# Softmax attention in slots of four heads and 64 queries, with the probabilities turned by VectorE in 32x32 squares

## The chip, the core and the metric

The program runs on one core of a Trainium2 chip. A core has five engines that work beside each other, each through its own instructions in their order: TensorE (PE in the profile, its weight loads PEld), VectorE (DVE), ScalarE (ACT), GpSimd (POOL) and SyncE (SP, which here only issues DMAs). TensorE reads SBUF and writes PSUM, which has eight banks of 512 fp32 values a partition; GpSimd works on SBUF alone here. The metric is the device time of one execution in microseconds (us). All data are fp32 but for one small bf16 product of the scan.

## The reference

Two residual blocks on x of shape (8, 1024, 512), eight sequences of 1024 tokens. The second block (a gated state-space scan) isn't touched by the change. The first one is modulated attention with 16 heads of 32 channels:

```python
x = x * s1[:, None, :]                                  # styles, then a norm over the channels
x = (x - mu) * rsqrt(var + EPS_IN)
q = heads((x @ q_weight.T) * q_dc);  k = heads((x @ k_weight.T) * k_dc)
v_flat = (x @ v_weight.T) * v_dc * s2;  v = heads(v_flat)
attn = softmax(einsum('bhqd,bhkd->bhqk', q, k) * d ** -0.5, axis=-1)
out = einsum('bhqk,bhkd->bhqd', attn, v)                # back to (B, S, H)
return (out @ w_weight.T) * w_dc + (v_flat @ u_weight.T) * u_dc      # x = x + this
```

## The kernel before

**Blocks and slots.** `modulated_attention` runs over 32 blocks (b, o): a sequence b and a group o of four heads, whose 4 x 32 channels fill the 128 partitions. `project` makes q, k and v of a block in a layout with channels on partitions and the 1024 tokens along the free axis. A block has 16 slots (`SB = 2 * NQ`), so there are 512. A slot is 128 queries (`q`, one of eight) of two of the four heads (`pair`).

**One slot.** `scores` (L292, L295) makes for each of the two heads a tile of 128 queries (on partitions) by 1024 keys, in two matmuls of 512 keys; a head has 32 channels, so a matmul uses 32 of TensorE's 128 rows. So that four matmuls use four different row groups, copies of q and k shifted by 64 partitions (`q2`, `k2`, made in `project` by DMAs on SP) serve the second 512 keys. The two tiles take four PSUM banks (`ps_s`), and the next slot takes the same ones. VectorE finds the negative maximum of each row (L465, one instruction for each head), ScalarE exponentiates with it as bias and adds up the rows (L475, one for each head), VectorE inverts the sums (`rinv`) and GpSimd multiplies the probabilities by them (L480, L489, L494).

**Turning.** The product with the values needs keys on partitions. One slot later `flip` turns each head's 128x1024 probabilities by eight TensorE transposes of 128x128 into PSUM (L302); ScalarE copies the first head's to SBUF (L472), VectorE the second's (L486, L491).

**Weighing.** Every second slot `weigh` (L309) takes the four heads of one q: for each of eight groups of 128 keys and each head one matmul with the head's 32 value channels as weights and the 128 turned probabilities moving, four column groups of TensorE beside each other. VectorE copies the result out (L454).

**Background work.** Between these, slots run pieces of generators: `project` for the next block, the output products `out_u` and `out_w` (all through `chain`, L136: four matmuls of 128x128x512 in a row, then an evacuation, by ScalarE for q, k and v, by VectorE for the outputs), the turning of the next x (`turn`) and its norm (`aside`). A piece is one matmul of a chain. `due` says how many pieces a slot owes (40 or 44 a block), and `late` how many of them come after the slot's own work. `turn_values` turns v by TensorE, and ScalarE copies it to `vt` (L237).

The order is written by hand (`tc.manual_schedule()`): every engine gets its instructions in the order of the code, and waits where a tile isn't ready. In fp32 a matmul of the code appears as two MATMUL and two LDWEIGHTS instructions in the profile (transposes as one of each).

After the attention, `gated_scan` runs the second block, with VectorE's custom step (L951), ScalarE's weighing (L929) and the DMAs that fan rows out (L919) as its largest parts.

Of the kernel before, what the change touches and what calls it, by code (L numbers as in the profile page):

```python
# [8 lines left out]
F32 = mybir.dt.float32  # L9
BF16 = mybir.dt.bfloat16  # L10
AF = mybir.ActivationFunctionType
ALU = mybir.AluOpType
AX = mybir.AxisListType
# [3 lines left out]
P = 128  # L17
# [4 lines left out]
HD = H // NH  # L22
# [7 lines left out]


@with_exitstack
def modulated_attention(ctx, tc, const, xp, tok, x1_d, xu_d, S, x, xT, cond, wT, ident, condT, early, handover):

# [6 lines left out]
    nc = tc.nc  # L43
    HW = S // 2
    KT = S // P
# [13 lines left out]
    eps = own.tile([P, 1], F32, name="eps_h")  # L59
    nc.vector.memset(eps, EPS)  # L60
    dc = own.tile([P, 5, KH, B], F32, name="dc")
    small = ctx.enter_context(tc.tile_pool(name="small", bufs=6))
    ps_m = ctx.enter_context(tc.tile_pool(name="ps_m", bufs=2, space=PSUM))

# [131 lines left out]
    def project(ws, xh, b, o, st, steps=STEPS):  # L196

        if not st:
            st["q"] = ring.tile([P, S], F32, tag="qT", name="qT")
            st["k"] = ring.tile([P, S], F32, tag="kT", name="kT")  # L200
            st["q2"] = ring.tile([P, S], F32, tag="q2", name="q2")
            st["k2"] = ring.tile([P, HW], F32, tag="k2", name="k2")
            st["v"] = ring.tile([P, S], F32, tag="vT", bufs=5, name="vT")
        qT, kT, q2, k2, vT = (st[n] for n in ("q", "k", "q2", "k2", "v"))

        def moved(dst, src):
            nc.sync.dma_start(out=dst[64:128], in_=src[0:64])
            nc.sync.dma_start(out=dst[0:64], in_=src[64:128])

        for name, hf in steps:  # L210
            c = half(hf)

            def q_out(ps):
                nc.scalar.mul(qT[:, c], ps, qdc[:, o, b : b + 1])
                moved(q2[:, c], qT[:, c])

            def k_out(ps):
                nc.scalar.mul(kT[:, c], ps, kdc[:, o, b : b + 1])
                if hf == 1:
                    moved(k2, kT[:, c])  # L220

            def v_out(ps):
                nc.scalar.mul(vT[:, c], ps, vdc[:, o, b : b + 1])
                ready.append((st, hf))

            out = {"q": q_out, "k": k_out, "v": v_out}[name]
            yield from chain([(ws[name][:, k], xh[hf][:, k]) for k in range(KH)], out)

    def turn_values():

        st, hf = ready.pop(0)
        if hf == 0:
            st["vt"] = ring.tile([P, KT, P], F32, tag="vt", name="vt")
        ps = ps_t.tile([P, 4, P], F32, tag="t", name="t_ps")
        for j in range(4):
            nc.tensor.transpose(ps[:, j], st["v"][:, (4 * hf + j) * P : (4 * hf + j + 1) * P], ident)
        nc.scalar.copy(st["vt"][:, 4 * hf : 4 * hf + 4], ps)  # L237

    def load_xr(src, o, hf):
        xr = ring.tile([P, HW], F32, tag="xr", bufs=3, name="xr")  # L240
# [39 lines left out]

    def scores(st, q, pair):


        s_ps = [ps_s.tile([P, S], F32, tag="s", name="s_ps") for _ in range(2)]
        qc = slice(q * P, (q + 1) * P)
        for hf in range(2):
            for i in range(2):
                if hf == 0:  # L290
                    r = slice(64 * pair + i * HD, 64 * pair + (i + 1) * HD)
                    nc.tensor.matmul(s_ps[i][:, 0:HW], st["q"][r, qc], st["k"][r, 0:HW], start=True, stop=True)  # L292
                else:
                    r = slice(64 * (1 - pair) + i * HD, 64 * (1 - pair) + (i + 1) * HD)
                    nc.tensor.matmul(s_ps[i][:, HW:S], st["q2"][r, qc], st["k2"][r], start=True, stop=True)  # L295
        return s_ps

    def flip(pr, g):
        ps = ps_t.tile([P, 4, P], F32, tag="t", name="t_ps")
        for j in range(4):  # L300
            c0 = (4 * g + j) * P
            nc.tensor.transpose(ps[:, j], pr[:, c0 : c0 + P], ident)  # L302
        return ps

    def weigh(av, pT, vt):
        for kt in range(KT):
            for i in range(4):
                r = slice(i * HD, (i + 1) * HD)
                nc.tensor.matmul(  # L309
                    av[r], vt[:, kt, r], pT[:, i, kt], start=(kt == 0), stop=(kt == KT - 1),  # L310
                    skip_group_check=True,
                )

    blocks = [(b, o) for b in range(B) for o in range(KH)]
    sts = {bo: {} for bo in blocks}
    slots = [(bo, q, pair) for bo in blocks for q in range(NQ) for pair in range(2)]
    wts = {}

    def fetch_w(n):
# [84 lines left out]
    def aside(n):  # L404

        b, o = blocks[n]
        if b + 1 < B and o in (1, 2):
# [2 lines left out]
            yield  # L410
            yield from normalise(xs_next[o - 1])

    xs_next, xh_next, last_w = [], [], []
    PIECES = {0: 40, 1: 40, 2: 44, 3: 44}
    probs = None
    flipped = {}
    bg, side, ran, ripe = iter(()), iter(()), 0, 0
    for n in range(len(slots) + 2):
        bo, q, pair = slots[n] if n < len(slots) else (None, None, None)
        if n % SB == 0:  # L420
            for _ in bg:
                pass
# [8 lines left out]
        if bo is not None:  # L431

            done, pieces = n % SB + 1, (54, 29)[n // SB] if n < 2 * SB else PIECES[bo[1]]
            few = max(1, (pieces - 2 * NQ + NQ) // SB)
            due = few * (done - done // 2) + -(-(pieces - NQ * few) * (done // 2) // NQ) - ran
            if n < 3:
                due = 6
            if n // SB == len(blocks) - 1:
# [3 lines left out]
            ran += due  # L442


        m = (n - 3) // 2
        if n % 2 == 1 and m >= 0:
            mbo, mq, _ = slots[2 * m]
            while "vt" not in sts[mbo] or (sts[mbo], 1) in ready:
                turn_values()
            av = ps_t.tile([P, 4, P], F32, tag="t", name="t_ps")[:, 0]  # L450
            weigh(av, flipped.pop(m), sts[mbo]["vt"])
            if mq == 0:
                sts[mbo]["a"] = ring.tile([P, S], F32, tag="aT", bufs=6, name="aT")
            nc.vector.tensor_copy(sts[mbo]["a"][:, mq * P : (mq + 1) * P], av)  # L454
        elif ripe and ready:
            turn_values()
        ripe = len(ready) if n % 2 == 1 else 0
        fresh = None
        if bo is not None:
            s_ps = scores(sts[bo], q, pair)  # L460
            nmax = [small.tile([P, 1], F32, name="nmax") for _ in range(2)]
            rsum = [small.tile([P, 1], F32, name="rsum") for _ in range(2)]
            fresh = [pp.tile([P, S], F32, name="pr") for _ in range(2)]
            for i in range(2):
                nc.vector.tensor_reduce(nmax[i], s_ps[i], AX.X, ALU.max, negate=True)  # L465
        if probs is not None:
            if (n - 1) % 2 == 0:
                flipped[(n - 1) // 2] = two.tile([P, 4, KT, P], F32, name="pT")
            pT = flipped[(n - 1) // 2][:, 2 * ((n - 1) % 2) : 2 * ((n - 1) % 2) + 2]
            t_ps = [flip(probs[0], g) for g in range(2)]  # L470
            for g in range(2):
                nc.scalar.copy(pT[:, 0, 4 * g : 4 * g + 4], t_ps[g])  # L472
        if bo is not None:
            for i in range(2):
                nc.scalar.activation(fresh[i], s_ps[i], AF.Exp, bias=nmax[i], accum_out=rsum[i])  # L475
        if bo is not None:
            rinv = [small.tile([P, 1], F32, name="rinv") for _ in range(2)]
            if n % 2 == 1:
                nc.vector.reciprocal(rinv[0], rsum[0])
                nc.gpsimd.tensor_scalar(fresh[0], fresh[0], rinv[0], 1.0, ALU.mult, ALU.mult)  # L480
        late = (due + 1 - n % 2) // 2
        for _ in range(due - late):
            next(bg, None)
        if probs is not None:
            t_ps = [flip(probs[1], g) for g in range(2)]
            nc.vector.tensor_copy(pT[:, 1, 0:4], t_ps[0])  # L486
        if bo is not None and n % 2 == 0:
            nc.vector.reciprocal(rinv[0], rsum[0])  # L488
            nc.gpsimd.tensor_scalar(fresh[0], fresh[0], rinv[0], 1.0, ALU.mult, ALU.mult)  # L489
        if probs is not None:  # L490
            nc.vector.tensor_copy(pT[:, 1, 4:8], t_ps[1])  # L491
        if bo is not None:
            nc.vector.reciprocal(rinv[1], rsum[1])  # L493
            nc.gpsimd.tensor_scalar(fresh[1], fresh[1], rinv[1], 1.0, ALU.mult, ALU.mult)  # L494
        for _ in range(late):
            next(bg, None)
        next(side, None)
        probs = fresh
    for _ in last_w[0]:
        pass  # L500

# [553 lines left out]
def network(ctx: ExitStack, tc: tile.TileContext, S, ins, out):  # L1055
# [22 lines left out]
    with tc.manual_schedule():  # L1078
        modulated_attention(
            tc, const, xp, tok, x1_d, xu_d, S, ins["x"], ins["xT"], ins["cond"],  # L1080
            {n: ins[f"w{n}T"] for n in "qkvwu"}, ident, ins["condT"], early, handover,
        )
        gated_scan(
            tc, const, tok, x1_d, S, win, tables, ins["w_conv"], ins["b_conv_c"], ins["ln_g"], ins["ln_b"],
# [78 lines left out]
```

## Time and profile before

| what | value |
|---|---|
| device time, median of 3 runs | 5662.0 us (5652.78 to 5665.36) |
| the profiled execution's own time | 5657.36 us |
| its span, first to last instruction | 5655.6 us |
| TensorE busy | 5502.6 us (97%), 43312 matmuls |
| VectorE busy | 4375.3 us (77%) |
| ScalarE busy | 3920.6 us (69%) |
| GpSimd busy | 1567.2 us (28%) |
| granted TensorE clock, mean | 0.99 |

The profile is one execution, taken by the hardware profiler. A line of a group says: source line, engine, operation, what it writes and reads, shapes, how often (xN), then the busy time in us and the mean ns of one, then the engine's idle time just ahead of such instructions and what ended most of it. A matmul's end is modelled and matmuls overlap, so their busy time is a union and their mean is longer than the distance from one to the next. In the timeline, a line is a run of instructions of one form: start, length of the run, and xN how many. The attention takes about the first 3270 us of the span, and the scan the rest.

### The profile page before, as it was taken

To read this page: it belongs to the slowest core of one execution; us is meant where nothing else is said; L and a number is where in the kernel's file an instruction comes from. 1 tells how busy PE (TensorE), PEld (TensorE's weight loads), DVE (VectorE), ACT (ScalarE), POOL (GpSimd) and SP (SyncE) were. 2 spreads that over 40 slices of the span, in tenths; PEclk is the share of its full clock that TensorE was granted. 3 is DMA by queue.
4 is the path that set the end of the run, shared out by engine and by line. 5 is a ranking of instruction groups with operands and counts; after the bars stand their busy time and mean duration, and the time that the engine had idled before them with its cause. 6 is when DMAs were issued, how large, how long until landed. Compare 5 with 4: busy or idle time off the path is not lost.

```text
span 5655.6 us, 113681 instructions
## 1 busy us (share of the span) xinstructions
PE 5502.6 (97%) x43312; PEld 3172.9 (56%) x43312; DVE 4375.3 (77%) x6847; ACT 3920.6 (69%) x6953; POOL 1567.2 (28%) x1723
## 2 busy tenths in 40 slices
PE   7999999999999999999999989999999999999998
PEld 4566666666666666666666555555555555555553
DVE  4676666766766767766766669999999999999996
ACT  5555555555555555555555558988888888889886
POOL 2443433433434434434333311111111111111111
PEclk9999999999999999999999989999999999999999
DMA  2111212112212202112111258888888888888886
GB/s 82 38 53 35 55 53 56 43 45 55 53 37 66 56 22 74 53 32 60 53 36 35 88 149 230 238 236 238 236 237 239 238 235 235 236 233 238 235 235 186
DMA packets 377214, 714.83 MB, mean 126 GB/s; under 512 B 198320, under 2 KB 280512, under 8 KB 347488
## 3 DMA queue, kind: packets, MB, share of 16 engines
q1 hardware_dynamic: 346704, 684.81, 44.3%
q0 software_dynamic: 29968, 22.77, 1.5%
q8 instruction: 344, 5.64, 0.4%
q14 instruction: 198, 1.62, 0.1%
HBM read 596.66 MB, written 83.89 MB: 120 GB/s over the span
## 4 chain that ended last, share of the span: by engine, by line
PE 66%; DMA 15%; DVE 9%; ACT 5%; SPq 3%; issue 2%; POOL 0%; DVEq 0%; ACTq 0%; POOLq 0%
PE mm_ps L136 18%; PE t_ps L302 15%; DMA xb<-xd 11%; PE s_ps L292 9%; PE t_ps L309 9%; DVE h L951 4%; PE in_ps L686 4%; PE y_ps L938 3%; SPq L919 3%; PE g_ps L841 2%; DMA xd<-xt 2%; ACT xb L929 2%; PE o_ps L878 1%; DMA out<-o_sb 1%; PE fan_ps L899 1%
## 5 line engine op out<-in xcount | busy, mean ns | idle before, releaser
L465 DVE TENSOR_REDUCE nmax<-s_ps 128x1 f32<-128x1024 f32 x1024 | 1205.5, 1219 | 464.5 <-PE s_ps L295 464.3
L951 DVE CUSTOM_DVE_ANT_0 h<-h,xb,lim 128x1024 f32<-128x1024 f32 x1024 | 1372.1, 1340 | 98.2 <-ACT xb L929 40.5
L472 ACT COPY pT<-t_ps 128x512 f32<-128x512 f32 x1024 | 550.6, 589 | 1294.2 <-PE t_ps L302 1294.2
L302 PEld LDWEIGHTS t_ps<-ident,pr 128*128 128x128 f32 x8192 | 915.9, 141 | 649.5 <-issue 500.1
L929 ACT ACTIVATE xb<-xb,ws 128x1024 f32<-128x1024 f32 x1024 | 1178.1, 1164 | 54.4 <-DMA xb<-xd 34.8
L475 ACT ACTIVATE pr<-s_ps,nmax 128x1024 f32<-128x1024 f32 x1024 | 1140.8, 1128 | 6.0 <-DVE nmax L465 5.9
L302 PE MATMUL t_ps<-ident,pr 128*128 128x128 f32 x8192 | 1094.0, 277 | 8.0 <-ACT pT L472 4.6
L494 POOL TENSOR_SCALAR pr<-pr,rinv 128x1024 f32<-128x1024 f32 x512 | 574.3, 1122 | 131.4 <-DVE rinv L493 121.8
L292 PE MATMUL s_ps<-kT,qT 32*128 32x512 f32 x2048 | 586.6, 640 | 3.1 <-ACT pr L475 2.4
L295 PE MATMUL s_ps<-k,q 32*128 32x512 f32 x2048 | 577.1, 639 | 1.1 <-DMA q<-qT 1.1
L480 POOL TENSOR_SCALAR pr<-pr,rinv 128x1024 f32<-128x1024 f32 x256 | 287.4, 1123 | 1035.3 <-PE t_ps L302 956.7
L938 PE MATMUL y_ps<-h,yw 128*32 128x512 f32 x4096 | 529.8, 613 | 36.2 <-DVE y_ps L773 32.4
L309 PEld LDWEIGHTS t_ps<-pT,vt 128*32 128x32 f32 x16384 | 433.2, 110 | 204.2 <-DVE rinv L488 164.5
L309 PE MATMUL t_ps<-pT,vt 128*32 128x128 f32 x16384 | 502.6, 275 | 10.9 <-DVE pT L486 9.2
L489 POOL TENSOR_SCALAR pr<-pr,rinv 128x1024 f32<-128x1024 f32 x256 | 287.5, 1123 | 792.6 <-DVE rinv L488 744.9
L686 PE MATMUL in_ps<-x,win 128*128 128x256 f32 x2048 | 491.9, 386 | 4.1 <-ACT xb L910 4.1
L841 PE MATMUL g_ps<-win,x1t 128*128 128x512 f32 x1024 | 472.2, 604 | 3.6 <-ACT x1t L836 3.6
L878 PE MATMUL o_ps<-wout,xt 128*128 128x512 f32 x1024 | 458.5, 595 | 0.0
L890 POOL DMA_DIRECT2D out<-o_sb x256 | 150.9, 595 | 1054.4 <-ACT o_sb L884 954.3
L686 PEld LDWEIGHTS in_ps<-x,win 128*128 128x128 f32 x2048 | 376.8, 193 | 95.0 <-ACT xb L910 26.5
L804 POOL DMA_DIRECT2D bca<-few x256 | 129.0, 513 | 1021.8 <-ACT few L797 1016.2
L486 DVE COPY pT<-t_ps 128x512 f32<-128x512 f32 x512 | 352.3, 688 | 48.0 <-PE t_ps L302 48.0
(162 smaller groups left out, 6961.0 us busy)
## 6 DMA issues: line engine op xcount, KB each, us to landing
xb<-xd SPq DMA_DIRECT2D x1792, 256.0 KB
xd<-xt SPq DMA_DIRECT2D x64, 512.0 KB
q<-qT SPq DMA_DIRECT2D x128, 128.0 KB
xr<-in_xT SPq DMA_DIRECT2D x64, 256.0 KB
xu_d<-xr SPq DMA_DIRECT2D x64, 256.0 KB
xr<-xu_d SPq DMA_DIRECT2D x64, 256.0 KB
x_d<-xr SPq DMA_DIRECT2D x64, 256.0 KB
out<-o_sb POOLq DMA_DIRECT2D x256, 64.0 KB, 4.7
```

The costliest lines, as they stand in the source:

```text
L136: nc.tensor.matmul(ps, w, x, start=(k == 0), stop=(k == KH - 1))
L292: nc.tensor.matmul(s_ps[i][:, 0:HW], st["q"][r, qc], st["k"][r, 0:HW], start=True, stop=True)
L295: nc.tensor.matmul(s_ps[i][:, HW:S], st["q2"][r, qc], st["k2"][r], start=True, stop=True)
L302: nc.tensor.transpose(ps[:, j], pr[:, c0 : c0 + P], ident)
L309: nc.tensor.matmul(av[r], vt[:, kt, r], pT[:, i, kt], start=(kt == 0), stop=(kt == KT - 1), skip_group_check=True,)
L465: nc.vector.tensor_reduce(nmax[i], s_ps[i], AX.X, ALU.max, negate=True)
L475: nc.scalar.activation(fresh[i], s_ps[i], AF.Exp, bias=nmax[i], accum_out=rsum[i])
L686: nc.tensor.matmul(ps, win[kk][:, k * P : (k + 1) * P], st["x1"][:, kk].rearrange("p b t -> p (b t)"), start=(kk == 0), stop=False,)
L841: nc.tensor.matmul(ps, st["xo", i][:, k], win[k][:, DI + half * 512 : DI + (half + 1) * 512], start=(k == 0), stop=(k == KH - 1),)
L929: nc.scalar.mul(xbs[n], xbs[n], sts[c]["ws"][:, t : t + 1])
L938: nc.tensor.matmul(st["y", i][32 * r : 32 * r + 32, hf * 512 : (hf + 1) * 512], yws[i][:, 4 * q + r, :], hs[4 * g + r][:, hf * 512 : (hf + ...
L951: nc.vector._custom_dve(dve_ops.TENSOR_ADD_SAT, out=h, in0=last["h"], in1=xbs.pop(n), s0=lim[:, 0, t : t + 1], s1=lim[:, 1, t : t + 1],)
```

## The change

A slot becomes 64 queries (`s`, one of sixteen) of all four heads; there are still 512 slots, with as many scores in each.

- `scores`: the 1024 keys of a head are taken as 32 groups of 32; groups 0, 2, 4, ... are one half, groups 1, 3, 5, ... the other. Partition group g of the score tile holds 32 of the 64 queries (g // 2) and one half of the keys (g % 2). A matmul has 32 channels, 32 queries and 512 keys; 16 of them (four row groups by four column groups of TensorE) make a slot. `q2`, `k2` and their DMAs go.
- A row's keys now lie on two partitions, so each has a maximum and a sum of its own. `factors` takes the difference of the two maxima by a matmul with a constant (`pair[:, 0]`) into the PSUM of the first score tile, VectorE clips it at 0, ScalarE exponentiates it and GpSimd multiplies the sums; `total` adds the two sums by a second matmul (`pair[:, 1]`) in the next slot; `shares` inverts there, and GpSimd scales the probabilities, one instruction for each head.
- `turn_probs`: VectorE turns the probabilities from SBUF to SBUF in squares of 32x32, two instructions of 128x1024 a slot. TensorE's transposes and the copies out of PSUM go.
- `weigh`: after turning, each query half has 64 partitions, with 32 keys of each key half. For each of 16 pairs of key groups, two query halves and four heads there is one matmul with 64 rows, 32 columns and 64 moving columns (32 queries of two slots); eight such matmuls lie on eight tiles of TensorE, two row groups by four column groups. Values shifted by 64 partitions (`vm`) come by two DMAs on SP for each `turn_values`.
- `due` and `late`, and the order of a slot's steps, change with it.

```diff
-    def scores(st, q, pair):
...
+    def scores(st, s):
+        s_ps = [ps_s.tile([P, 2, HW], F32, tag="s", name="s_ps") for _ in range(2)]
+        for g in range(4):
+            half_q, half_k = divmod(g, 2)
+            q0 = 64 * s + HD * half_q
+            for h in range(4):
+                r = slice(h * HD, (h + 1) * HD)
+                keys = st["k"][r].rearrange("p (j a k) -> p a j k", a=2, k=HD)[:, half_k]
+                nc.tensor.matmul(
+                    s_ps[h // 2][g * HD : (g + 1) * HD, h % 2], st["q"][r, q0 : q0 + HD], keys, start=True, stop=True
+                )
         return s_ps
-    def flip(pr, g):
...
+    def weigh(av, pT, st):
+        for j in range(2 * KT):
+            for r in range(2):
+                rows = slice(64 * r, 64 * r + 64)
+                v = st["vt" if j % 2 == r else "vm"]
+                for h in range(4):
+                    c = slice(h * HD, (h + 1) * HD)
+                    nc.tensor.matmul(
+                        av[r][c, 0:64], v[rows, j // 2, c], pT[rows, h, :, j * HD : (j + 1) * HD],
+                        start=(j == 0), stop=(j == 2 * KT - 1), skip_group_check=True,
+                    )
...
+    def limits(ch, i):
+        if i == 0:
+            ch["nmax"] = small.tile([P, 4], F32, name="nmax")
+            ch["sum"] = small.tile([P, 4], F32, name="rsum")
+        for h in ((0, 1), (1, 2)) if i == 0 else ((0, 2),):
+            nc.vector.tensor_reduce(
+                ch["nmax"][:, 2 * i + h[0] : 2 * i + h[1]], ch["s"][i][:, h[0] : h[1]], AX.X, ALU.max, negate=True
+            )
+    def powers(ch, i):
+        ch["p", i] = pp.tile([P, 2, HW], F32, name="pr")
+        for h in range(2):
+            c = slice(2 * i + h, 2 * i + h + 1)
+            nc.scalar.activation(
+                ch["p", i][:, h], ch["s"][i][:, h], AF.Exp, bias=ch["nmax"][:, c], accum_out=ch["sum"][:, c]
+            )
+    def factors(ch):
+        d_ps = ch["s"][0][:, 0, 0:4]
+        nc.tensor.matmul(d_ps, pair[:, 0], ch["nmax"], start=True, stop=True)
+        f = ch["f"] = small.tile([P, 4], F32, name="fac")
+        nc.vector.tensor_scalar_min(f, d_ps, 0.0)
+        nc.scalar.activation(f, f, AF.Exp)
+        nc.gpsimd.tensor_tensor(ch["sum"], ch["sum"], f, ALU.mult)
+    def total(ch):
+        ps = ch["tot"] = ps_t.tile([P, HW], F32, tag="t", name="tot_ps")
+        nc.tensor.matmul(ps[:, 0:4], pair[:, 1], ch["sum"], start=True, stop=True)
+    def shares(ch):
+        g = small.tile([P, 4], F32, name="share")
+        nc.vector.reciprocal(g, ch["tot"][:, 0:4])
+        nc.gpsimd.tensor_tensor(g, g, ch["f"], ALU.mult)
+        for h in range(4):
+            p = ch["p", h // 2][:, h % 2]
+            nc.gpsimd.tensor_scalar(p, p, g[:, h : h + 1], 1.0, ALU.mult, ALU.mult)
+    def turn_probs(n, i):
+        if n % 2 == 0 and i == 0:
+            flipped[n // 2] = two.tile([P, 4, 2, HW], F32, tag="pT", name="pT")
+        nc.vector.transpose(flipped[n // 2][:, 2 * i : 2 * i + 2, n % 2], chains[n]["p", i])
...
-            few = max(1, (pieces - 2 * NQ + NQ) // SB)
-            due = few * (done - done // 2) + -(-(pieces - NQ * few) * (done // 2) // NQ) - ran
+            due = -(-pieces * (5 * done + done % 2) // (5 * SB)) - ran
...
+        late = due // 3
+        if n - 2 in chains:
+            turn_probs(n - 2, 1)
+        fresh = None
+        if bo is not None:
+            fresh = chains[n] = {"s": scores(sts[bo], s)}
+        if n - 1 in chains:
+            total(chains[n - 1])
+        if bo is not None:
+            limits(fresh, 0)
+        if n - 1 in chains:
+            shares(chains[n - 1])
+        if bo is not None:
+            limits(fresh, 1)
+            for i in range(2):
+                powers(fresh, i)
+        for _ in range(due - late):
+            next(bg, None)
...
-            av = ps_t.tile([P, 4, P], F32, tag="t", name="t_ps")[:, 0]
-            weigh(av, flipped.pop(m), sts[mbo]["vt"])
...
+            av = [ps_t.tile([P, HW], F32, tag="t", name="av_ps") for _ in range(2)]
+            weigh(av, flipped.pop(m), sts[mbo])
...
         if bo is not None:
+            factors(fresh)
+        if n - 1 in chains:
+            turn_probs(n - 1, 0)
+        if av is not None:
+            if ms == 0:
+                sts[mbo]["a"] = ring.tile([P, S], F32, tag="aT", bufs=6, name="aT")
+            rows = sts[mbo]["a"].rearrange("p (s r q) -> p r s q", r=2, q=HD)
+            for r in range(2):
+                nc.scalar.copy(rows[:, r, ms : ms + 2], av[r][:, 0:64].rearrange("p (s q) -> p s q", q=HD))
         for _ in range(late):
             next(bg, None)
```

## The prediction

> **What bounds the kernel now.** I read the busy times by stage first, then one pair of slots in TensorE's timeline, then the groups, then the waits. By stage (columns: window, its length, then busy us and count of PE, PEld, DVE, ACT, POOL, then granted clock, DMA share, GB/s), the attention and one of its steady blocks of 16 slots:
>
> ```profile
> 60.00:3260.00 3200.00, 3156.63 (x31544) 1938.38 (x31542) 2176.28 (x3605) 1844.42 (x3355) 1273.34 (x1189) 1.00 0.18 50
> 1370.40:1468.40 98.00, 97.90 (x985) 59.81 (x985) 69.31 (x116) 57.08 (x104) 45.34 (x45) 1.00 0.26 71
> ```
>
> TensorE is busy 97.90 of 98.00 us at full clock, VectorE 69.31, ScalarE 57.08. The block gives 6.13 us a slot. The maxima of L465, two a slot, number 1020 in those 3200 us: 6.27 us a slot over the whole stage, 12.55 a pair. One pair of slots on TensorE:
>
> ```profile
> 1505.72 0.70 PE L292 MATMUL s_ps<-kT,qT 32*128 32x512 f32 x2
> ...
> 1506.79 1.09 PE L302 MATMUL t_ps<-ident,pr 128*128 128x128 f32 x8
> 1507.72 1.02 PE L136 MATMUL mm_ps<-xh,w_k 128*128 128x512 f32 x2
> 1508.58 1.04 PE L302 MATMUL t_ps<-ident,pr 128*128 128x128 f32 x8
> 1509.45 1.02 PE L136 MATMUL mm_ps<-xh,w_k 128*128 128x512 f32 x2
> 1510.40 1.96 PE L309 MATMUL t_ps<-pT,vt 128*32 128x128 f32 x64
> 1512.29 0.70 PE L292 MATMUL s_ps<-kT,qT 32*128 32x512 f32 x2
> ```
>
> From start to start: scores 1.07, eight transposes 0.93 or 0.87, a piece of a chain 0.86, a weighing 1.89. A pair has 2 x 1.07 + 4 x 0.9 + 5 x 0.86 + 1.89 = 11.9, and with the turned values about 12.1: TensorE sets the pace. The rows that the change touches:
>
> ```profile
> L465 DVE TENSOR_REDUCE nmax<-s_ps 128x1 f32<-128x1024 f32 x1024 | 1205.5, 1219 | 464.5 <-PE s_ps L295 464.3
> ...
> L472 ACT COPY pT<-t_ps 128x512 f32<-128x512 f32 x1024 | 550.6, 589 | 1294.2 <-PE t_ps L302 1294.2
> ...
> L475 ACT ACTIVATE pr<-s_ps,nmax 128x1024 f32<-128x1024 f32 x1024 | 1140.8, 1128 | 6.0 <-DVE nmax L465 5.9
> ...
> L494 POOL TENSOR_SCALAR pr<-pr,rinv 128x1024 f32<-128x1024 f32 x512 | 574.3, 1122 | 131.4 <-DVE rinv L493 121.8
> ...
> L486 DVE COPY pT<-t_ps 128x512 f32<-128x512 f32 x512 | 352.3, 688 | 48.0 <-PE t_ps L302 48.0
> ...
> L766 ACT ACTIVATE sq_ps<-xt 128x512 f32<-128x512 f32 x128 | 75.5, 590 | 58.8 <-DVE xt L755 58.8
> ```
>
> VectorE and ScalarE wait for TensorE (464.3 and 1294.2 us), hardly the other way: before ScalarE's exponentials there are 6.0 us.
>
> **The change on TensorE.** Out: four groups of transposes, 3.6 us a pair. In: four small matmuls (`factors`, `total`). A 128-column load takes 0.11 a pass, a fp32 matmul has two, and a change of tile shape costs about 0.1 (the last scores' half starts at 1506.26, streams 0.43, and the next load comes at 1506.79): 0.33 each, 1.3 a pair.
>
> Scores: four matmuls on four row groups took 1.07. Sixteen tiles with 512 moving columns stream as long if all run at once; the staggered starts add what the shorter loads (32 columns instead of 128) save: 1.1. Lower bound 0.95; upper 1.9, if only eight run at once.
>
> Weighing is the main unknown. Before, 64 instructions with 128 columns ran in waves of four, 16 waves in 1.89: 0.11 a wave. Now there are 256 with 64 columns. If eight tiles run at once, that is 32 waves of 0.055, 1.76, with entry and drain 1.98. But instructions must then start 6.9 ns apart, load and matmul together, for almost 2 us. How fast can they start?
>
> ```profile
> 1512.07 0.29 PE L309 MATMUL t_ps<-pT,vt 128*32 128x128 f32 x4
> ...
> 3757.13 0.19 PEld L938 LDWEIGHTS y_ps<-h,yw 128*32 128x32 f32 x8 [1.20 <-PE in_ps L690]
> 3757.16 0.64 PE L938 MATMUL y_ps<-h,yw 128*32 128x512 f32 x4 [0.84 <-DVE y_ps L773]
> ```
>
> Four matmuls of 0.275 each fill 0.29: they start within 0.02, about 6 ns apart. In the scan, after a wait, eight loads and four matmuls start within 0.1. So bursts are fast enough, by a hair; a sustained burst isn't shown. Bounds: below, 1.8; above, if the two row groups follow each other, 64 waves, 3.7; farthest, at the 29 ns per instruction of the old weighing, 7.5. I take 1.98, since the nearest rows are the staggered starts.
>
> The Trainium skill speaks against this part ("TensorE: Matmul & The Clock Gate", section "Wait — 56ns, not 53.3ns?"): from one matmul's start to the next it never sees less than about 25 ns, however few the columns. By that rule the weighing would take 256 x 25 = 6.4 us and the run some 1,100 us more. The rows above show starts of 6 ns between different tiles, so I don't apply it.
>
> So TensorE falls to 2.2 + 1.3 + 4.3 + 2.0 = 9.8 a pair. What is late next is VectorE.
>
> **The change on VectorE.** Out a slot: two copies (0.69 + 0.68), a second reciprocal, half an L454 (0.15). In: two squares-turnings of 128x1024. No row shows one. The reduction of as many elements takes 1.22, and consecutive ones start 1.14 to 1.18 apart; the scan's one-pass 128x1024 row, L951, takes 1.34. I take 1.23, starts 1.17 apart; bounds 1.07 (elements alone: twice the 0.54 by which L475's 1024 take longer than L766's 512) and 2.3 (two passes). The skill's "Vector Engine (DVE) Microarchitecture Reference", section 3.8, states one element per cycle and lane for it, by which the sum below stands; no run here shows it.
>
> The maxima: two of 512 (0.61 apart, as the copies of L486 and L491 start when they follow each other) and one of 1024: 2.4. Minimum 0.15, reciprocal 0.1. Background from its groups (L257, L273, L90, L91, L121: 172 us over 512 slots): 0.34. Sum 2.4 + 2.34 + 0.25 + 0.34 = 5.3 a slot, against 4.3.
>
> **A new chain.** The scores have no second buffer: scores(n+1) wait for the last exponential and for the minimum of slot n; that minimum waits for `factors` on TensorE, which stands behind pieces and weighing, and behind the waiting minimum VectorE queues both next turnings and so the next maxima. Around a pair, from the even slot's last maximum:
>
> - handoff 0.05, two exponentials of 512 with their sums (0.6 + 0.74), handoff 0.05: 1.44;
> - odd slot on TensorE: scores 1.1, `total` 0.33, two pieces 1.72, weighing 1.98, `factors` till visible 0.45, handoff 0.05: 5.63;
> - VectorE: minimum 0.15, turning 1.17, background about 0.25, turning 1.17, maxima with reciprocal 0.61 + 0.61 + 0.1 + 1.22: 5.28.
>
> That is 12.35 against 12.55: 0.2 x 256 = 51 us less. (VectorE alone, 2 x (5.3 + 0.5 for the wait on `factors`) = 11.6, is the floor.)
>
> **At nothing.** ScalarE: four exponentials, the small one, copies of `av`, values and evacuations, about 3.5 a slot of 6.1; GpSimd: four scalings of about 0.6 and two small ones, 2.8, with the norm's steps up to 4.1. Both lie beside VectorE and begin to count past 6.1. `total` waits for GpSimd's product of the sums, with the pieces and the weighing queued behind it: that is ready about 0.7 after the minimum (small exponential 0.25, product 0.2, three handoffs), while the scores ahead of it take 1.1; each 0.1 past that would be 0.1 a pair. It also takes the PSUM bank that ScalarE's copies of `av` must free, some 0.1 late in even slots, where VectorE covers it. `q2`/`k2` go: their waits were 1.1 us in all. Four `vm` DMAs a block replace six on SP's queue, and weight loads queue behind them as before; values are turned slots ahead of their first use. Without that cover a landing (4.7 us, `out<-o_sb`) a block would be 150 us. The scan doesn't change.
>
> The profiled execution took 5657.4 (span 5655.6), 4.6 below the median. 5657.4 - 51 + 4.6 = **5611**. Its own range is 5560 to 5660 (0.2 us a pair either way). About 0.2%, 11 us, is what a measurement of this kernel can tell from no change.
>
> **Rivals.**
>
> 1. *Weighing becomes the bound (slower).* It decides at 1.98 + 0.2 = 2.18 us, a wave of 61 ns instead of 55. For: no row shows such dense issue, nor row and column groups together. Against: the 6 ns starts. At a wave of 75 ns it is 2.6, +0.62 a pair, 5770; with row groups in turn 3.7, 6050. Chance 0.30.
> 2. *Turning takes two passes.* VectorE alone then takes 7.8 a slot: some 6400; at 1.4 us, +0.46 a pair, 5730. For: no row. Against: every fp32 row shows about 1 ns an element. 0.08.
> 3. *The sixteen score tiles don't all run at once.* Scores 1.9; in the odd slot all of 0.8 counts, in the even half is hidden: +0.8 to 1.2 a pair, 5820 to 5920. 0.06.
> 4. *The chain is hidden better,* pairs between VectorE's floor of 11.6 (5420) and 12.1 (5545), in the middle 5490. For: handoffs are rounded up. Against: the chain has no slack for anything forgotten. 0.10.
>
> **How the numbers follow.** The forecast has 0.46. Of it 0.38 is faster, 0.05 the same, 0.03 slower. With rival 4, faster is 0.48; rival 1 gives 0.02 to the same, all else is slower: 0.07 and 0.45. The range 5510 to 5880 leaves out about 0.06 below (half of rival 4) and 0.13 above (the far ends of 1 and 2).
>
> **What would show it.** Right: x256 in L309's place about 2.0 us long, 32 score matmuls in 1.1, turnings of 1.2 us, VectorE above 85% in the attention, its largest wait `factors` on TensorE, pairs of about 12.3. Wrong: a weighing above 2.2 us, turnings above 1.35, scores above 1.3, or GpSimd waited for.

## The result, and the profile after

The changed kernel takes 6538.1 us (median of 4 runs, 6534.1 to 6551.2) against 5662.2 us (4 runs): a ratio of 1.155, 95% interval 1.153 to 1.158. The forecast was 5611, its range 5510 to 5880; the change is slower by 876 us, far outside it. The profiled execution took 6534.2 us, its span 6532.4.

By stage first, as before (window, length, busy us and count of PE, PEld, DVE, ACT, POOL, granted clock, DMA share, GB/s): the attention, and the 98 us that were shown of the kernel before.

```profile
60.00:4140.00 4080.00, 3400.31 (x86728) 1748.40 (x86726) 2620.85 (x3870) 1725.66 (x5405) 1716.78 (x3235) 0.88 0.14 39
1370.40:1468.40 98.00, 81.02 (x2040) 42.54 (x2040) 63.99 (x98) 38.79 (x124) 41.49 (x79) 0.85 0.19 56
```

No engine is full. TensorE is busy 81 of 98 us where it had 97.90, VectorE 64, and the granted clock is down to 0.85 from 1.00. By the starts of each slot's first maximum, a slot now takes 7.98 us and a pair 15.95, against 6.27 and 12.55; 512 slots of 1.7 us more are some 870 of the 876 us, so the scan hardly moved. The slots are uneven: even ones take 6.31, odd ones, which hold the weighing, 9.66.

The rows that answer to those of before:

```profile
L304 PE MATMUL av_ps<-pT,vt 64*32 64x64 f32 x32640 | 769.0, 230 | 232.9 <-issue 231.7 <-DVE share L445 0.8 <-DVE pT L456 0.2
L304 PE MATMUL av_ps<-pT,vm 64*32 64x64 f32 x32640 | 725.2, 231 | 246.7 <-issue 223.4 <-DVE share L445 16.3 <-ACT vt L232 3.0
...
L414 DVE TENSOR_REDUCE nmax<-s_ps 128x1 f32<-128x512 f32 x1533 | 1250.0, 842 | 73.4 <-PE s_ps L290 73.3
L456 DVE STREAM_TRANSPOSE pT<-pr 128x1024 f32<-128x1024 f32 x1022 | 1217.3, 1222 | 0.8 <-DVE fac L433 0.8
L449 POOL TENSOR_SCALAR pr<-pr,share 128x512 f32<-128x512 f32 x2044 | 1379.8, 697 | 50.3
...
L433 DVE TENSOR_SCALAR fac<-s_ps 128x4 f32<-128x4 f32 x512 | 82.7, 161 | 1341.1 <-PE s_ps L431 1341.1
```

The turning takes 1222 ns, as reckoned. VectorE waits 1341 us for the small matmul of `factors`, which stands behind the weighing. And in the weighing, TensorE itself stands 455 us for "issue": it waits for nothing that the profile shows. One weighing from close by, TensorE's rows around its pause:

```profile
1002.74 0.29 PE L304 MATMUL av_ps<-pT,vt 64*32 64x64 f32 x8
1002.80 0.24 PE L304 MATMUL av_ps<-pT,vm 64*32 64x64 f32 x1
1002.81 0.27 PE L304 MATMUL av_ps<-pT,vt 64*32 64x64 f32 x4
1004.91 0.29 PE L304 MATMUL av_ps<-pT,vm 64*32 64x64 f32 x8 [1.83 <-issue]
```

In mid-weighing, with all operands there, no instruction starts from 1002.86 to 1004.91. The DMA view of 1002.40 to 1006.00, in 40 slices of 0.09 us, has a single transfer, and it is of instructions:

```profile
GB/s 0 182 0 0 0 0 0 0 0 0 0 0 0 0 0 0 0 0 0 0 0 0 0 0 0 0 0 0 0 0 0 0 0 0 0 0 0 0 0 0
DMA packets 1, 0.02 MB, mean 5 GB/s; under 512 B 0, under 2 KB 0, under 8 KB 0
...
q8 instruction: 1, 0.02, 1.8%
```

The second slice is the start of this packet (16,384 bytes). Its record begins at 1002.52 and lasts 1.01 us; TensorE goes on 1.38 us after its end. This is no single case. The trace has 228 pauses of over 0.8 us inside weighings, 513 us in all, and in 9 of 10 TensorE resumes 1.22 to 1.59 us after the end of an instruction packet, median 1.38. With 680 packets in the attention's 4076 us, one every 6 us, chance would put one in sixteen into that band. The place of the pauses says the same: with TensorE's records (matmuls, loads and the few of its sequencer) numbered in order of start, 218 of the 228 pauses stand at the same place of every 256 instructions, where chance would put one. The page counts the packets of the whole run, here after the change and then before it:

```profile
q8 instruction: 777, 12.73, 0.9%
```
```profile
q8 instruction: 344, 5.64, 0.4%
```

### The profile page after: what moved, and what is told of

It reads as the page before. It is cut to its first block, busy times and chain, and to the rows that moved or that the text cites. A ratio compares the mean times of both kernels' runs of the same rounds, so it can differ in the third digit from the quotient of the medians.

```text
span 6532.4 us, 227679 instructions
## 1 busy us (share of the span) xinstructions
PE 5733.5 (88%) x98608; PEld 2977.0 (46%) x98608; DVE 4815.9 (74%) x7103; ACT 3799.8 (58%) x9001; POOL 2009.9 (31%) x3771
## 4 chain that ended last, share of the span: by engine, by line
PE 50%; DVE 15%; DMA 15%; issue 10%; ACT 7%; SPq 2%; POOL 0%; DVEq 0%; ACTq 0%; POOLq 0%
PE mm_ps L138 15%; PE av_ps L304 12%; DMA xb<-xd 11%; PE s_ps L290 10%; DVE pT L456 5%; DVE h L985 4%; DVE nmax L414 3%; ACT pr L423 3%; PE in_ps L720 3%; PE s_ps L431 2%; PE y_ps L972 2%; SPq L953 2%; PE tot_ps L440 2%; DMA xd<-xt 2%; ACT xb L963 2%
## 5 line engine op out<-in xcount | busy, mean ns | idle before, releaser
L423 ACT ACTIVATE pr<-s_ps,nmax 128x512 f32<-128x512 f32 x2048 | 1380.5, 686 | 1613.8 <-DVE share L445 1590.7
L985 DVE CUSTOM_DVE_ANT_0 h<-h,xb,lim 128x1024 f32<-128x1024 f32 x1024 | 1373.1, 1341 | 99.4 <-ACT xb L963 50.7
L449 POOL TENSOR_SCALAR pr<-pr,share 128x512 f32<-128x512 f32 x2048 | 1382.5, 697 | 50.4
L414 DVE TENSOR_REDUCE nmax<-s_ps 128x1 f32<-128x512 f32 (+1 forms) x1536 | 1252.4, 842 | 84.4 <-PE s_ps L290 84.3
L456 DVE STREAM_TRANSPOSE pT<-pr 128x1024 f32<-128x1024 f32 x1024 | 1219.8, 1222 | 2.7 <-POOL pr L449 1.8
L304 PE MATMUL av_ps<-pT,vt 64*32 64x64 f32 x32768 | 773.5, 231 | 238.9 <-issue 231.7
L304 PE MATMUL av_ps<-pT,vm 64*32 64x64 f32 x32768 | 729.1, 231 | 248.8 <-issue 225.5
L290 PE MATMUL s_ps<-kT,qT 32*32 32x512 f32 x16384 | 880.5, 738 | 74.5 <-issue 66.3
L304 PEld LDWEIGHTS av_ps<-pT,vt 64*32 64x32 f32 x32768 | 598.1, 107 | 437.9 <-issue 342.2
L304 PEld LDWEIGHTS av_ps<-pT,vm 64*32 64x32 f32 x32768 | 573.8, 107 | 279.7 <-issue 243.7
L440 PEld LDWEIGHTS tot_ps<-rsum,pair 128*128 128x128 f32 x1024 | 184.4, 225 | 563.8 <-issue 283.7
```

Of the source, the lines that this page charges most:

```text
L290: nc.tensor.matmul(s_ps[h // 2][g * HD : (g + 1) * HD, h % 2], st["q"][r, q0 : q0 + HD], keys, start=True, stop=True)
L304: nc.tensor.matmul(av[r][c, 0:64], v[rows, j // 2, c], pT[rows, h, :, j * HD : (j + 1) * HD], start=(j == 0), stop=(j == 2 * KT - 1), skip ...
L414: nc.vector.tensor_reduce(ch["nmax"][:, 2 * i + h[0] : 2 * i + h[1]], ch["s"][i][:, h[0] : h[1]], AX.X, ALU.max, negate=True)
L423: nc.scalar.activation(ch["p", i][:, h], ch["s"][i][:, h], AF.Exp, bias=ch["nmax"][:, c], accum_out=ch["sum"][:, c])
L449: nc.gpsimd.tensor_scalar(p, p, g[:, h : h + 1], 1.0, ALU.mult, ALU.mult)
L456: nc.vector.transpose(flipped[n // 2][:, 2 * i : 2 * i + 2, n % 2], chains[n]["p", i])
```

## The experiments

The theory, A: TensorE outruns the supply of its instructions. Rivals: B, the tiles of 64 rows take turns or stream slower than reckoned; C, the order, since VectorE waits for `factors` behind the weighing; D, every instruction costs TensorE its share wherever it stands.

| kernel | time, us | us a slot | weighing, first to last start, mean us |
|---|---|---|---|
| before | 5662 | 6.27 | 1.69 |
| changed | 6538 | 7.98 | 4.77 |
| half_instr | 5762 | 6.47 | 1.95 |
| half_stream | 6468 | 7.87 | 4.45 |
| before_split | 6721 | 8.35 | 5.86 |
| factors_first | 6818 | 8.52 | 5.26 |
| woven | 6413 | 7.72 | 5.29 with the piece inside |
| split_weigh | 5827 | 6.58 | 2 x 1.46 |
| split_fill | 6787 | 8.43 | 2 x 2.58 |
| split_early | 5939 | 6.82 | 2 x 1.93 |
| split_early_fill | 5856 | 6.66 | 2 x 1.73 |
| split_even | 5726 | 6.40 | 2 x 1.73 |
| even | 5713 | 6.37 | 2 x 1.48 |
| even_fill | 5651 | 6.26 | 2 x 1.44 |

half_instr, half_stream, before_split and factors_first are single runs beside one of the kernel before, 5660; the others have three rounds or more, and 95% intervals of about 0.2% either way.

**Half the instructions, the same columns (half_instr).**

```diff
-        for j in range(2 * KT):
+        for j in range(0, 2 * KT, 2):
...
-                        av[r][c, 0:64], v[rows, j // 2, c], pT[rows, h, :, j * HD : (j + 1) * HD],
+                        av[r][c, 0:128], v[rows, j // 2, c], pT[rows, h, :, j * HD : (j + 2) * HD],
...
```

> The changed kernel with half the matmuls in each weighing and twice the moving columns in each: 8 instead of 16 key groups, 128 instead of 64 columns, so the columns streamed are the same. It leaves out the products of every second group of keys. Theory A (supply of instructions: 256 of them come in one 16 KB packet, two packets never started less than 3.3 us apart in the changed kernel's trace, and a weighing takes 512 of them at once): the weighing now takes 256, one packet; the stalls inside it vanish, a pair of slots falls from 15.95 us to near the 12.35 us of the prediction's sum, 5600 to 5900 us. Rival B (the tiles of 64 rows take turns or the streaming itself is slower than the 0.055 us a wave of the prediction): the columns are the same, the time stays at 6400 to 6550. Rival C (the order: VectorE's minimum waits behind the weighing for the small matmul, and the chain turns late): the same matmul still stands behind the weighing; 6300 to 6550.

5761.9 us: 776 less, as theory A has it. Of the groups, the weighing (idle time behind the second bar), and the page's count of packets:

```profile
L304 PE MATMUL av_ps<-pT,vt 64*32 64x128 f32 x16256 | 522.2, 275 | 0.8 <-DVE share L445 0.8
L304 PE MATMUL av_ps<-pT,vm 64*32 64x128 f32 x16256 | 519.3, 276 | 14.8 <-DVE share L445 9.8 <-ACT vt L232 2.9 <-issue 1.4
```
```profile
q8 instruction: 521, 8.54, 0.6%
```

The 455 us for which these matmuls waited for issue are 1.4. A wave of eight tiles, 128 columns, takes 0.109 us and the median weighing 1.76: eight tiles of 64 rows run at once, at the price that the prediction set for the streaming. Rival B is out. The kernel has 65,536 instructions and 256 packets fewer, so a packet is 256 instructions, and queue 8 brings TensorE's. The Trainium skill ("Runtime: NRT & Kernel Launch", section "Instruction fetch mechanics") gives these 16 KiB blocks too, and calls the cost of crossing one mostly hidden; the size agrees, but in the changed kernel's trace the crossing costs 2 us a weighing, and there the measurement decides.

**The same instructions, half the columns (half_stream).**

```diff
-                        av[r][c, 0:64], v[rows, j // 2, c], pT[rows, h, :, j * HD : (j + 1) * HD],
+                        av[r][c, 0:32], v[rows, j // 2, c], pT[rows, h, 0, j * HD : (j + 1) * HD],
...
```

> The changed kernel with all 128 matmuls in each weighing, each over 32 moving columns instead of 64 (one slot's columns are weighed and written twice, the other's left out). Theory A (supply of instructions): the same 512 instructions, so 6300 to 6550 us, though half of the streaming is gone. Rival B (streaming, or tiles in turns): about half of the 4.8 us that a weighing spans goes, 2.4 us x 256 pairs = 610 us: 5850 to 6050.

6468 us: half of the streaming gone buys 70 us. The pauses stay (226 over 0.8 us, 537 us in all). Between them a matmul starts every 8.3 ns in the median, against 9.8 in the changed kernel and 6.9 in the prediction: a wave of eight takes 67 ns where 32 columns would stream in 27 (a quarter of half_instr's 0.109), so with so few columns the pace is that of the instructions and not of the columns. The skill's 25 ns from start to start ("TensorE: Matmul & The Clock Gate", section "Wait — 56ns, not 53.3ns?") is not seen here, with the matmuls on eight tiles in turn.

**The old weighing cut in four (before_split).**

```diff
-                nc.tensor.matmul(
-                    av[r], vt[:, kt, r], pT[:, i, kt], start=(kt == 0), stop=(kt == KT - 1),
-                    skip_group_check=True,
-                )
+                for c in range(0, P, HD):
+                    nc.tensor.matmul(
+                        av[r, c : c + HD], vt[:, kt, r], pT[:, i, kt, c : c + HD],
+                        start=(kt == 0), stop=(kt == KT - 1), skip_group_check=True,
+                    )
```

> The kernel before, with each matmul of its weighing cut into four of 32 moving columns: same products, same order, same columns streamed, but 512 instructions in a weighing instead of 128. Theory A: a pair of slots takes about 2.4 packets instead of 0.9, and two of them in one burst: 1.5 to 3 us more for each of 256 pairs, 6050 to 6450 us. Rival B and rival C (tiles of 64 rows; order of the new chain), neither of which this kernel has: 5640 to 5750.

6721 us, beyond the range of theory A, though 384 packets more, as counted. (It starts four sums in one bank, one after another, and part of the products seems to be lost by that; instructions and columns are as said.) The weighing takes 5.86 us in place of 1.69, and 256 x 4.17 = 1068 us is all of the 1062. But most of it is no pause: 32 matmuls take 0.613 us in the median all along, 19 ns each, at a granted clock of 0.99. Pauses of over 0.8 us come to 122 us; all 84 end 1.19 to 1.61 us after a packet, and they stand at one place of every 256 instructions. So this run shows that cutting matmuls into 32 columns is dear with none of the new tiles and none of the new chain, and that pauses for packets come with it; it doesn't show that the packets are the main cost here. What sets 19 ns for tiles of 128 rows, when tiles of 64 rows start every 8 to 10, stayed open. One rival wasn't tried: the four cuts of a matmul follow each other on the same column group, so that eight matmuls of the profile in a row use one tile, where the kernel before has two.

**The small matmul ahead of the weighing (factors_first).** The two lines of `factors` move from behind the weighing to just before it.

> The changed kernel with the small matmul of the maxima, its minimum, exponential and product issued ahead of the weighing instead of behind it. Rival C (the chain of a slot is late because VectorE waits for that matmul behind the weighing, 1328 us of wait in the changed kernel's trace): most of the extra goes, 5650 to 5900 us. Theory A: the weighing starves as before and TensorE sets the pace, 6350 to 6550 us.

6818 us, slower than either theory said. VectorE's largest waits on TensorE:

```profile
DVE nmax L414 <- PE s_ps L290: 1166.5, 244, 10.2
...
DVE fac L433 <- PE s_ps L431: 382.1, 455, 3.2
```
```profile
PEld s_ps L431 <- ACT pr L423: 749.1, 454, 3.5
```

The wait at the minimum fell from 1341 to 382 us, and a new one of 1167 us stands before the maxima: TensorE now stands for the small matmul's operands (749 us on its loads, for ScalarE), the weighing starts later, the next scores wait behind it. The wait was a symptom, and half_instr, which keeps the order, had got 776 us back: rival C is out as the cause.

**One piece of other work in the middle (woven).**

```diff
...
-            weigh(av, flipped.pop(m), sts[mbo])
+            weigh(av, flipped[m], sts[mbo], range(KT))
+            for _ in range(kept):
+                next(bg, None)
+            weigh(av, flipped.pop(m), sts[mbo], range(KT, 2 * KT))
```

> The changed kernel, whole result, all 512 instructions of a weighing in its odd slot and into the same sums, with one of the slot's 128x512 matmul pieces (1.1 us, four instructions) moved from ahead of the weighing to its middle. Theory A (a packet of 256 instructions takes 3.3 us or more to follow the last): the two halves lie 1.1 us further apart, so the stall of 2.2 us a weighing shrinks by about that: 250 to 300 us less than the 6538 us, 6200 to 6350. Rival D (each instruction costs its share wherever it stands): nothing changes, 6480 to 6580 us.

6413 us, a gain of 126: less than the 190 to 340 that theory A promised, more than rival D allows. The median pause fell from 2.25 to 1.17 us, by the 1.1 that the piece lasts, and the pauses over 0.8 us inside the two halves from 513 to 297 us; 126 us show in the time (and the mean clock rose from 0.92 to 0.96). So a pause is a delay that other work can cover in part.

**Two bursts instead of one (split_weigh).**

```diff
-        for j in range(2 * KT):
+        for j in range(part * KT, (part + 1) * KT):
...
-        if n % 2 == 1 and m >= 0:
+        if m >= 0:
...
+                if n % 2 == 1:
+                    nc.scalar.copy(part, a)
+                else:
+                    more = small.tile([P, 2, HD], F32, name="more")
+                    nc.scalar.copy(more, a)
+                    nc.gpsimd.tensor_tensor(part, part, more, ALU.add)
...
```

> The changed kernel, whole result, with the same 512 instructions of a weighing issued in two bursts: key groups 0 to 7 in the odd slot, 8 to 15 in the next even slot, whose sums ScalarE copies out and GpSimd adds to the first half's. Theory A (a burst outruns the packets of 256 instructions): a burst now takes one packet, the stalls go, each burst takes near 1.25 us (128 matmuls by the 9.8 ns that the unstalled middle of a weighing shows), and the time comes near that of the kernel with half the instructions, 5762 us: 5720 to 5900. Rival D (each instruction costs TensorE its share wherever it stands, 4.8 us per 256 matmuls): nothing is saved, 6450 to 6600 us.

5827 us, ratio 1.029 (1.027 to 1.031) to the kernel before: 711 of the 876 us come back with every instruction kept, and even some added. Rival D is out. A burst takes 1.27 us in the median. Of pauses over 0.8 us inside weighings 27 are left, 34 us in all.

**What is left (split_fill, split_early, split_early_fill, split_even, even, even_fill).** These start from split_weigh.

> As split_weigh, and VectorE's wait for the small matmul of the maxima is filled: that matmul writes a bank of its own (so that it no longer waits for the exponentials that read the bank it shared) and stands ahead of the weighing, and VectorE turns the second half of the slot before last between the maxima and the minimum (five buffers of probabilities instead of four). Theory A with the chain as what is left: the 1.2 us a slot that VectorE waits at the minimum in the kernel with half the instructions (628 us over 512 slots) falls to 0.5 or less, 0.3 to 0.7 us a slot less than split_weigh: 5450 to 5650 us. Rival C' (the chain is not what sets the pace once the stalls are gone, TensorE is): within 60 us of split_weigh.

6787 us: the worst of the line, for the reason of factors_first. The minimum is ahead of the weighing, the weighing of the scores, and VectorE waits 1194 us for scores:

```profile
DVE nmax L414 <- PE s_ps L290: 1194.3, 394, 7.7
```

> As split_weigh (5827 us), with TensorE's order in a slot changed: one piece of the chains of 128x512 matmuls, then the half weighing, then the small matmul of the maxima, and the rest of the pieces behind it; in split_weigh two thirds of the pieces and the weighing stood ahead of that matmul. VectorE's minimum comes earlier (in split_weigh it waits 586 us for it), and the pieces cover ScalarE's exponentials. Theory: once the bursts are small, the chain scores, maxima, small matmul, turning sets the pace: 0.3 to 0.6 us a slot less, 5520 to 5680 us. Rival (TensorE's own work sets the pace, whatever its order): within 40 us of split_weigh.

5939 us, 111 slower instead of 150 to 300 faster. VectorE's wait at the minimum fell from 586 to 453 us, but its wait for scores rose from 127 to 311. With the weighing first, TensorE also stands (200 us on its loads, 39 in split_weigh) for VectorE's reciprocal; I take it that this frees the bank.

> As split_early, with the turning of a slot's second half moved behind the next but one slot's maxima, where VectorE would wait for the small matmul, the weighing one slot later, and five buffers of probabilities. If VectorE's chain (5.2 us of work a slot and its waits) sets the pace, 0.2 to 0.4 us a slot less than split_early, 5400 to 5600 us; if scores, maxima and the four exponentials of a slot do (0.65 + 1.25 + 4 x 0.89 and the steps between, about 5.8 us), the same as split_early within 40 us.

5856 us, 82 less than split_early: 0.16 us a slot, between the two answers. Even slots took 7.43 us and odd ones 5.89. The pieces were still dealt as if every second slot held the whole weighing, which split_early had inherited too.

> As split_early_fill (5856 us), with the background pieces dealt out evenly over the slots (they stood 3 and 2, as the whole weighing lay in every second slot) and the turning of the values put right behind the scores, where ScalarE is idle, instead of behind its copies. Even slots took 7.43 us and odd ones 5.89 there. If TensorE's own work sets the pace (about 6.1 us a slot by its pieces, scores, weighing and small matmuls), the mean of 6.66 falls to 6.2 to 6.4 and the time to 5600 to 5720 us; if something else does, it stays within 40 us.

5726 us, 131 less, just above the range: slots of 6.72 and 6.09.

> split_weigh (5827 us) with the background pieces dealt out evenly over the slots and the turning of the values right behind the scores, and nothing else: order of TensorE (two thirds of the pieces, half weighing, small matmul, rest) and place of the turnings as in the changed kernel. In split_weigh even slots took 6.89 us and odd ones 6.26. If the pace is set by TensorE's work, both come to 6.25 to 6.35: 5640 to 5710 us. If by VectorE's wait for the small matmul behind the weighing (586 us in split_weigh), it stays above split_even's 5726.

5713 us, just outside both answers; slots of 6.45 and 6.29. VectorE still waits 581 us at the minimum, yet it is no slower than split_even.

> split_even (5726 us) with the order of pieces of the changed kernel (two thirds ahead of the half weighing, the rest behind the small matmul) instead of one ahead and the rest behind. If TensorE sets the pace and stands idle at the small matmul and at the scores in turn, 5640 to 5720 us and within 30 us of the kernel called even; if the pieces behind the small matmul are what covers the exponentials, it is 30 to 100 us slower than split_even.

5651 us, inside the range of the first answer, but further from even than its 30 us. Ratio 0.9986 (0.9976 to 0.9996): 62 us faster than even, and level with the kernel before, since 0.14% is less than what counts as a difference here. Its attention:

```profile
60.00:3260.00 3200.00, 2993.62 (x86481) 1554.88 (x86479) 2662.37 (x3871) 1776.79 (x5911) 1855.10 (x3743) 0.98 0.18 49
```
```profile
PEld av_ps L304 <- issue: 386.6, 509, 2.8
DVE nmax L414 <- PE s_ps L290: 334.6, 453, 7.4
```

TensorE is busy 2994 of 3200 us, at a clock of 0.98 again, and VectorE 2662. Only this kernel of the line has, beside the small bursts, all three of these: VectorE's turning in the wait, two thirds of the pieces ahead of the half weighing, and the pieces dealt evenly. Its weighings still wait 387 us for issue, on the loads, 0.76 us each time and about once a burst; what that costs, no run shows. No kernel here beats the one before by more than a measurement can tell.

## Why the prediction was wrong

**The step that failed** is the weighing, taken at 1.98 us a pair, and with it the supply of instructions, which no term held. From its first start to that of the next work, which is how the 1.89 of the kernel before was read, it takes 4.96, so 2.98 us x 256 = 763 of the 927 us between forecast and result. From first to last start (4.77) it has two parts:

- The pace between pauses: 10.6 ns from start to start in the mean instead of 6.9, that is 2.69 us for 256. The 6 ns came from bursts of four to eight instructions, and the text said itself that a sustained burst wasn't shown. The trace of before couldn't show one: its densest 32 instructions of TensorE in a row, loads included, take 0.36 us, 11 ns each, where the sum needed 3.4.
- The pauses: those over 0.5 us come to 532 us over 256 weighings, 2.08 us each. Nobody had priced these: the prediction asked how fast instructions can start, but not how fast they come. The profile before had the row (344 packets) and the count of instructions; 512 instructions in 2 us against a packet about every 13 us in the attention was to be read off, as a risk if not as a size.

**Rival 1** had the direction, the place and the point of decision (2.18 us) right, at a chance of 0.30. Its causes were not what happened: row groups don't take turns. Its wave of 75 ns, worth 2.6 us, was close: the unstalled wave has 75 ns in the median and 85 in the mean. But the pauses came on top, and 4.96 us lies between its 3.7 and the 7.5 put as the farthest bound, outside the range that was given.

**The chain** was put at 12.35 us a pair. half_instr, whose weighing takes 2.15 us to the start of the next work, comes to 12.95. VectorE's own work in it is 5.12 us a slot (2613.76 us over 510 slots) where 5.3 was reckoned; its idle time is 1.35 where the sum left 0.88. So, beside 0.17 of the weighing, 0.43 a pair, 110 us, went to waits that were mis-sized. One of them is large: the small matmul shares a bank with scores that ScalarE still reads, and in half_instr TensorE waited for that on its loads:

```profile
PEld s_ps L431 <- ACT pr L423: 516.9, 256, 3.4
```

That this wait is the 0.43, no run isolates. 12.35 + 2.98 + 0.43 = 15.76 of the measured 15.95; the last 0.2 was not taken apart, and the clock may lie in it. Matmuls of 128x512 show 683 to 721 ns in the changed kernel and 626 to 649 in half_instr.

**What held.** Scores at full clock: the 32 starts lie within 0.61 us in the median, sixteen tiles at once, and 1.20 us with the last stream, where 1.1 was reckoned; rival 3 is out. But over all 512 sets the medians are 0.88 and 1.46: 78 sets ran wholly at half clock and took 2.33, 71 of them right behind a weighing, and that was in no term. Turning: 1222 ns against 1.23 us; rival 2 is out. Maxima: 2.45 us against 2.4. GpSimd's scaling takes 697 ns instead of 600 and stays beside. `factors` is VectorE's largest wait on TensorE, as foretold, and VectorE is busy 64% instead of the 85 foretold, since TensorE holds the pace back.

## What to carry to other kernels

Count the instructions of a burst, not only its columns: small tiles turn streaming time into instructions, and 512 of them in a row cost 4.8 us here where their columns cost 1.8. By the places where the pauses stand, 235 of 257 blocks of 256 instructions that ran in under 2.9 us left a pause of over 0.3 us behind them in the changed kernel (60 to 3300 us), but 8 of 59 in half_instr, where a burst is one block long: a lone fast block mostly passes. Waits for "issue" in the middle of work whose operands are there, and resumptions a fixed time after a packet on the instruction queue, name the cause; spread the burst over other work, or make each matmul stream more columns. A large wait on another engine (VectorE's 1341 us) may be a mere consequence: moving the awaited matmul forward made it worse.

## What the runs showed of the hardware

- An instruction packet is 16,384 bytes and 256 instructions. In the attention of these kernels two of them never started less than 3.2 us apart; nine of ten pauses of the changed kernel end 1.22 to 1.59 us after the packet's end, about 2.4 us after its start. Pauses stand at one place of every 256 instructions: 218 of 228 in the changed kernel, 291 of 294 in factors_first.
- In the changed kernel the packet that ends a pause starts about 1.0 us (median, pauses of over 0.3 us at that place) after TensorE has begun the 256 instructions ahead of the pause, and TensorE goes on 3.5 us after having begun them. The 256 themselves take 1.28 us; the pause is the rest, 2.24. In half_stream the same three are 3.4, 1.08 and 2.28 us, in before_split 3.2, 2.46 and 0.68.
- Those packets lie a median of 4.8 us behind the one before them, in before_split 9: so it is not the least distance of 3.2 us alone that holds them back, but when they are sent. Why a packet isn't sent earlier no run shows.
- Matmuls of 64x32 on eight tiles in turn start every 8.3 ns (32 columns) to 9.8 ns (64 columns) in long bursts, tiles of 128x32 with 32 columns, eight on one tile in a row, every 19 ns.
- TensorE's granted clock was 1.00 in the attention before, 0.88 in the changed kernel, 0.95 in half_instr, 0.98 in even_fill. In the changed kernel, between 60 and 4000 us, 170 of the 182 times that it falls to half come within 6 us of the start of a time of over 1.5 us in which no matmul runs; there are 231 such times. In half_instr, with hardly a pause inside its weighings, 69 of 78 do so too. No run here changes the idle time alone.
